# A two-pass feed-forward layer: ScalarE's order written out, more places for its activations, its first two blocks prepared inside attention

## The chip, the cores and the metric

The kernel runs on one core of a Trainium2 chip. The metric is the device time of one execution in microseconds (us). The engines of the core are called by the names that the profile uses: PE (TensorE, matmul; PEld is its weight load), DVE (VectorE), ACT (ScalarE), POOL (GpSimd) and SP (SyncE, which issues DMAs). Each engine works through its own queue in order and waits on semaphores that other engines raise. PE writes to PSUM, which has eight banks of 128 x 512 words; in what follows a "bank" is one of these.

## The reference, cut to what matters

The input is x of 4 batches x 1024 tokens x 128. Four layers follow one another, each added to x, each on a layer norm of x:

1. an attention layer with 16 heads,
2. a feed-forward layer with ternary weights, the one that the change rewrites,
3. a gated linear attention, which first needs a decay for each token,
4. a mixture of experts, of which three of eight are taken for each batch.

```python
def _L0_ffn_ref(x, w1_w, w1_s, w2_w, w2_s, h1_w, h1_s, h2_w, h2_s, w3_w, w3_s):
    h = jax.nn.silu(_tlin(x, w1_w, w1_s)) * _tlin(x, w2_w, w2_s)
    h = jax.nn.gelu(_tlin(h, h1_w, h1_s), approximate=False)
    h = jax.nn.gelu(_tlin(h, h2_w, h2_s), approximate=False)
    return _tlin(h, w3_w, w3_s)          # _tlin: x @ w.T * s
# 128 -> 512 (w1, w2), 512 -> 512 (h1), 512 -> 512 (h2), 512 -> 128 (w3)
# decay of the layer after it, from the x that this layer leaves:
gk = jax.nn.log_sigmoid(x @ Wgk1 @ Wgk2 + bgk2) / 16
```

## The kernel before, in words

**Attention.** Its scores are worked off in 16 sets of 16 steps. In each step PE makes two tiles of maxima (`mx`) for the set after, two tiles of scores (`sc`) and the weighted sums (`oacc`); DVE reduces the maxima (`nm`, L367), ACT takes the exponential (`pr`, L564). PE's order is the order of the program text (`manual_schedule`), that of the other engines is chosen by a scheduler. Small pieces of other work go into two queues, `after` and `ahead`, and `others()` (L514) takes at most one piece that needs PSUM per step. All these pieces share one bank (`misc`). Before each half of a batch, `prepare` norms, turns and projects its tokens; the projection (L290) keeps a tile under the tag `raw`, of which there are two places. In the last half there is nothing left to prepare, and `turn_pieces` turns the weights of the feed-forward layer there.

**The two-pass layer** (`ffn0_rounded`, L673) runs after a branch on a flag. Ternary weights are exact in a rounded format, so each activation is split into a high part (`*_hi`, a rounded copy) and a low part (`*_lo`, the rest), and each product is made twice. The 4096 tokens are 8 blocks of 512. For each block there are

- `turn` (L718): norm, four transposes (`tps`), `x_hi` on ACT, `x_lo` on DVE;
- `gates` (L736): for each of four column groups 4 matmuls, tanh on ACT (`sg`, L743), two products on DVE (`sg`, L744, and `h`, L746), `h_hi` on ACT, `h_lo` on POOL;
- `hidden` (L757), once for h1 and once for h2: 32 matmuls into four banks, then four gelus on ACT (`g`, L766) with two places for `g`, `g_hi` on ACT for groups 0 and 2 and on DVE for 1 and 3, `g_lo` on POOL for groups 0 to 2 and on DVE for 3;
- `down` (L777): 8 matmuls, `yT` on ACT, and later four transposes (`yps`, L812) and the sum into x;
- `behind`, the decays of the next layer (`gla_decay`, L1014), in three pieces: `turn` (norm, transposes `dps`, copy `h_nat`), `rank` (`lps`, `lr` on ACT), `decays` (`zps`, `low` on DVE, then absolute value on ACT, and for every second block an exponential and a logarithm of 1024 columns, a subtraction on POOL and two scans on DVE, `g_sum`).

Seven banks hold the matmul results of `gates`, `hidden` and `down`. One bank (`ps_t`, tag `turn`) is shared by `tps`, `yps`, `dps`, `lps` and `zps`.

The loop is skewed. Iteration k makes h2 of block k, h1 of block k+1, w3 of block k and the gates of block k+2. The small pieces wait in a queue `later`, and `hidden` takes one of them after each quarter of its matmuls. So an iteration from 1 to 5 has `yps`, `tps`, nothing, `dps` in h2 and nothing, `lps`, nothing, `zps` in h1. The pieces that come from block k-1 make iterations 2, 4 and 6 "heavy" (they hold the exponential and logarithm of a whole batch); 1, 3 and 5 are "light". Iteration 7 and the tail behind the loop each have the exponential and logarithm of half a batch. PE's order is the program's; ACT, DVE and POOL are ordered by the scheduler.

Of the kernel before, what the change touches and what calls it, by code (L numbers as in the profile page):

```python
# [9 lines left out]
F32 = mybir.dt.float32  # L10
# [14 lines left out]
class Block:  # L25
# [35 lines left out]
    def load_later_weights(self):  # L61
# [3 lines left out]
        for name in ("w1", "w2", "h1", "h2", "w3"):  # L65
# [9 lines left out]
            for name, t in self.ffn0_w.items()  # L75
        }
        self.same = self.ctile([P, 512], "same")
        nc.gpsimd.memset(self.same, 1.0)
# [45 lines left out]
    def turn_pieces(self, bank):  # L124
# [14 lines left out]
        for name, nat in self.ffn0_w.items():  # L139
            for ic in range(nat.shape[2] // P):  # L140
                out.append(
                    lambda k=len(out), nat=nat, dst=self.ffn0_r[name], ic=ic: piece(k, nat, dst, ic)
                )
        return out

    def set_flag(self, work, bank):
# [38 lines left out]
    def attention(self):  # L185
# [7 lines left out]
        with ExitStack() as ctx:  # L193
# [330 lines left out]
            for s, (hf, i) in enumerate(sets):  # L524
                cur = halves[hf]
                if i == 0 and hf + 1 < n_half:
                    halves[hf + 1], todo = prepare(hf + 1)
                    for piece in todo:
                        ahead.append(piece)
                        if hf > 0 and piece[0] and compare:  # L530
                            ahead.append((0, compare.pop(0)))
                elif i == 0:
                    ahead.extend((1, f) for f in self.turn_pieces(misc))
                    ahead.append((1, lambda: self.set_flag(work, misc)))
                qf = cur["q"][:, i].rearrange("p c t -> p (c t)")
# [42 lines left out]
            weighted(pend)  # L578
            while after:
                after.popleft()[1]()  # L580

# [91 lines left out]
    def ffn0_rounded(self, behind):  # L673
# [7 lines left out]
        with ExitStack() as ctx:  # L681
# [3 lines left out]
            ps_m = ctx.enter_context(tc.tile_pool(name="r_psm", bufs=7, space=PSUM))  # L685
            ctx.enter_context(tc.manual_schedule(engines={mybir.EngineType.PE}))

# [48 lines left out]
            def gates(x2):  # L736
                out = []
                for oc in range(FC):
                    gate, val = bank(), bank()
                    products("w1", {oc: gate}, x2, 0, 1)  # L740
                    products("w2", {oc: val}, x2, 0, 1)
                    sg = work.tile([P, TB], F32, name="sg", tag="sg")
                    nc.scalar.activation(sg, gate, AF.Tanh, scale=half[:, oc : oc + 1])  # L743
                    nc.vector.scalar_tensor_tensor(sg, sg, 1.0, gate, ALU.add, ALU.mult)  # L744
# [10 lines left out]
            later = deque()  # L755

            def hidden(name, src):  # L757
                out = {oc: bank() for oc in range(FC)}
                for ic in range(FC):
                    products(name, out, src[ic], ic, FC)  # L760
                    if later:
                        later.popleft()()
                res = []
                for oc in range(FC):
                    g = work.tile([P, TB], F32, name="g", tag="g")
                    nc.scalar.activation(g, out[oc], AF.Gelu, scale=col(name, oc))  # L766
# [10 lines left out]
            def down(blk, g):  # L777
# [4 lines left out]
                nc.scalar.mul(yT, ps[0], col("w3", 0))  # L782
                return [lambda: self.add_turned(ps_t, yT, 4 * blk), lambda: None] + behind(blk, ps_t)
# [38 lines left out]
    def gla(self):  # L822
# [3 lines left out]
        with ExitStack() as ctx:  # L826
# [83 lines left out]
            for b in range(B):  # L910
# [15 lines left out]
                for a in range(4):  # L926
                    qhs = []
                    for jq in range(4):
                        j = 4 * jq + a
                        kv = work.tile([P, S], F32, name="kv", tag="kv")  # L930
                        for hb in range(NH):
# [9 lines left out]
                            nc.vector.tensor_tensor(kv[:, cols], vr, kT[:, cols], ALU.mult)  # L941
                        hs = work.tile([P, S], F32, name="hs", tag="hs")
                        nc.vector.tensor_tensor_scan(hs, dec, kv, 0.0, ALU.mult, ALU.add)
# [70 lines left out]
    def gla_decay(self, blk, pool, ps_pool):  # L1014
# [48 lines left out]

        return [turn, lambda: None, rank, lambda: None, decays]

# [460 lines left out]
```

## Time and profile before

| what | us |
|---|---|
| median of three runs (1667.61 to 1690.93) | 1667.72 |
| the profiled execution | 1665.73 |
| its span, from the first to the last instruction | 1664.0 |
| of it, attention and what leads up to it, to the last `ctxT` product at 982.3 | 982 |
| the two-pass layer with the decays, 982.3 to 1282.5 | 300 |
| the gated linear attention and the experts | 381 |

The views of the profile show one execution. Times count from the start of the span. A row of the timeline is a start, a length, the engine, the line, the operation with its tiles, and in brackets the idle time ahead of it with what ended it. A row of the windows is the stretch, its length, the busy time of each engine with its number of instructions, and the PE clock that was granted (1.00 is full), the share of the DMA engines and the GB/s moved.

### The profile page before, as it was taken

To read this page: it belongs to the slowest core of one execution; us is meant where nothing else is said; L and a number is where in the kernel's file an instruction comes from. 1 tells how busy PE (TensorE), PEld (TensorE's weight loads), DVE (VectorE), ACT (ScalarE), POOL (GpSimd) and SP (SyncE) were. 2 spreads that over 40 slices of the span, in tenths; PEclk is the share of its full clock that TensorE was granted. 3 is DMA by queue.
4 is the path that set the end of the run, shared out by engine and by line. 5 is a ranking of instruction groups with operands and counts; after the bars stand their busy time and mean duration, and the time that the engine had idled before them with its cause. 6 is when DMAs were issued, how large, how long until landed. Compare 5 with 4: busy or idle time off the path is not lost. (4 is left out here: it accounts for less than half of the span.)

```text
span 1664.0 us, 25053 instructions
## 1 busy us (share of the span) xinstructions
PE 1400.1 (84%) x10256; PEld 712.5 (43%) x10256; DVE 1068.9 (64%) x1863; ACT 843.9 (51%) x1053; POOL 490.0 (29%) x469
## 2 busy tenths in 40 slices
PE   1599887799898998998989969979774878679998
PEld 1343333334343343433433326656551544445554
DVE  3688795689898897988988736643442555532220
ACT  0056663466666666666666645555544323153332
POOL 4434066525051150421500016544442000201110
PEclk9999997899999999999999989979895987789999
DMA  5000000000000000000000000000000000101110
GB/s 140 4 2 1 1 1 1 0 2 2 1 2 1 2 2 1 1 1 1 2 1 1 1 1 0 1 1 1 0 0 2 1 1 1 30 10 51 51 51 15
DMA packets 23247, 16.06 MB, mean 10 GB/s; under 512 B 9536, under 2 KB 20432, under 8 KB 23120
## 3 DMA queue, kind: packets, MB, share of 16 engines
q1 hardware_dynamic: 15792, 7.99, 1.7%
q0 software_dynamic: 1920, 6.29, 1.4%
q8 instruction: 84, 1.38, 0.4%
q10 hardware_dynamic: 5408, 0.05, 0.2%
q14 instruction: 43, 0.35, 0.1%
HBM read 12.23 MB, written 2.10 MB: 9 GB/s over the span
## 5 line engine op out<-in xcount | busy, mean ns | idle before, releaser
L564 ACT ACTIVATE pr<-sc 128x1024 f32<-128x1024 f32 x512 | 518.1, 1026 | 321.9 <-PE sc L556 272.1
L367 DVE TENSOR_REDUCE nm<-mx 128x2 f32<-128x1024 f32 x512 | 612.8, 1219 | 106.1 <-PE sc L556 57.6
L360 PE MATMUL mx<-k,q 32*128 32x512 f32 x1024 | 264.1, 516 | 53.6 <-ACT pr L564 40.3
L477 PE MATMUL oacc<-pr,vaug 128*32 128x512 f32 x2048 | 280.8, 617 | 0.0
L547 PE MATMUL sc<-q,k 32*128 32x512 f32 x1024 | 251.6, 502 | 22.7 <-DVE nm L367 21.0
L547 PEld LDWEIGHTS sc<-q,k 32*128 32x128 f32 x1024 | 95.4, 185 | 291.2 <-issue 107.2
L556 PE MATMUL sc<-mT,a_ones 32*128 32x512 f32 x1024 | 201.8, 394 | 0.0
L360 PEld LDWEIGHTS mx<-k,q 32*128 32x128 f32 x1024 | 97.3, 189 | 127.0 <-ACT pr L564 105.1
L165 POOL TENSOR_TENSOR ln_rs<-ln_rs,mhalf 128x4 f32<-128x4 f32 (+2 forms) x44 | 42.5, 967 | 313.2 <-DVE ln_rs L164 312.8
L1459 ACT ACTIVATE g<-up 128x512 f32<-128x512 f32 x96 | 56.7, 597 | 105.3 <-PE up L1451 105.2
L1451 PE MATMUL up<-mT,wa 128*128 128x512 f32 x192 | 97.8, 599 | 0.4 <-DVE att_s L1207 0.4
L556 PEld LDWEIGHTS sc<-mT,a_ones 32*128 32x128 f32 x1024 | 97.6, 189 | 0.6 <-ACT mT L378 0.2
L1441 PE MATMUL zT<-g,wb 128*128 128x512 f32 x192 | 97.4, 602 | 0.0
L773 POOL TENSOR_TENSOR g_lo<-g,g_hi 128x512 fp32r<-128x512 f32 x48 | 65.4, 1375 | 73.0 <-ACT g_hi L771 60.0
L386 POOL COPY mxpad<-mhi 128x16 f32<-128x16 f32 x32 | 6.8, 212 | 263.4 <-PE sc L556 179.0
L769 DVE CAST g_hi<-g 128x512 fp32r<-128x512 f32 x32 | 16.9, 528 | 94.8 <-ACT g L766 94.8
L314 POOL TENSOR_SCALAR raw<-raw,wq_take 128x512 f32<-128x512 f32 x32 | 50.2, 1569 | 82.8 <-DVE hi L313 81.5
L1451 PEld LDWEIGHTS up<-mT,wa 128*128 128x128 f32 x192 | 58.6, 309 | 31.8 <-issue 19.4
L477 PEld LDWEIGHTS oacc<-pr,vaug 128*32 128x32 f32 x2048 | 41.4, 108 | 70.2 <-issue 68.2
L766 ACT ACTIVATE g<-mm,h_s 128x512 f32<-128x512 f32 x64 | 42.3, 687 | 56.6 <-POOL g_lo L773 29.1
L314 POOL TENSOR_SCALAR raw<-raw,wk_take 128x512 f32<-128x512 f32 x32 | 50.5, 1579 | 33.4 <-DVE hi L313 33.4
L710 PE MATMUL mm<-g_hi,h_r 128*128 128x512 f32 x128 | 47.3, 475 | 10.6 <-DVE sg L744 4.6
(244 smaller groups left out, 2004.8 us busy)
## 6 DMA issues: line engine op xcount, KB each, us to landing
xs<-in_L_attn_x SPq DMA_DIRECT2D x8, 256.0 KB
h_nat<-in_L_ffn_h_w SPq DMA_DIRECT2D x2, 1024.0 KB
out<-xs SPq DMA_DIRECT2D x8, 256.0 KB
w_nat<-in_L_ffn_w_w SPq DMA_DIRECT2D x3, 256.0 KB
bq<-in_L_attn_bq ACTq DMA_DIRECT2D x16, 0.5 KB
bk<-in_L_attn_bk ACTq DMA_DIRECT2D x16, 0.5 KB
gWo<-in_L_attn_Wo SPq DMA_DIRECT2D x16, 4.0 KB
wa<-in_L_ffn_Wa,at_i POOLq DMA_INDIRECT x12, 3.7
```

The lines of the kernel that those rows point to most:

```text
L314: nc.gpsimd.tensor_scalar(raw, raw, take[key], None, ALU.mult)
L360: nc.tensor.matmul(ps[:, jj, :], qf[32 * j : 32 * j + 32, ch * P : (ch + 1) * P], kf[32 * j : 32 * j + 32, kh * KH : (kh + 1) * KH], start ...
L367: nc.vector.tensor_reduce(nm[:, kh, ch, 2 * jp : 2 * jp + 2], ps, AX.X, ALU.max, negate=True)
L477: nc.tensor.matmul(pend["oacc"][32 * j : 32 * j + 32, :], pend["v"][:, j, pend["ch"], :], pend["p"][j // 2][:, j % 2, :], start=pend["ch"] ...
L547: nc.tensor.matmul(ps[:, jj, :], kf[rows, ch * P : (ch + 1) * P], qf[rows, qh * KH : (qh + 1) * KH], start=True, stop=False,)
L556: nc.tensor.matmul(ps[:, jj, :], ones[rows, :], mT[rows, qh * KH : (qh + 1) * KH], start=False, stop=True,)
L564: nc.scalar.activation(pr, ps, AF.Exp, scale=scale)
L710: nc.tensor.matmul(ps, wT[name][:, ic, oc * P : (oc + 1) * P], half, start=ic == 0 and h == 0, stop=ic == n_ic - 1 and h == 1,)
L773: eng.tensor_tensor(g2[1], g, g2[0].bitcast(F32), ALU.subtract)
L1441: nc.tensor.matmul(zT, zones[k][1][:, fc * E : (fc + 1) * E], g, start=n == 0, stop=n == len(steps) - 1,)
L1451: nc.tensor.matmul(ps, zones[k][0][:, fc, :], xT[:, hb * TB : (hb + 1) * TB], start=True, stop=True,)
L1459: nc.scalar.activation(g, ps, AF.Gelu_apprx_tanh)
```

## The change

Five things are done.

1. In `ffn0_rounded` ACT, too, runs in the order of the program text.
2. `sg` gets three places instead of two, `h` four instead of two, `g` five instead of two. In `gates` the split of h into high and low part is put off by two column groups.
3. The queue `later` is gone. h2 of iteration k takes `yps` (of block k-1) after its first quarter and `dps` after its fourth; h1 takes `tps` (for block k+2) after its first quarter, `lps` after its second and `zps` with all that follows after its fourth. In the last iteration `lps` and `zps` come ahead of w3.
4. The norm, turn and split of blocks 0 and 1 move into the last half of attention (`first_pieces`), into four tiles of their own. Their normed tiles use the tag `raw`. In the queue `ahead` the two norms stand first, then the 14 turns of weights, then the two turns and the flag. Behind the last set both queues are emptied.
5. In `gla`, which stands on the side of a branch that is not taken here, `kv` and `hs` get one place instead of two.

```diff
+    def first_pieces(self, work, bank):
+        nc, out = self.nc, []
+        for blk, x2 in enumerate(self.first_x):
+            src = self.xs[:, 4 * blk : 4 * blk + 4, :]
+            got = {}
+            def norm(src=src, got=got):
+                mv, rs = self.norm_stats(work, src, 4)
+                got["xn"] = xn = work.tile([P, 4, E], F32, name="xn", tag="raw")
+                for k in range(4):
+                    self.norm_apply(xn[:, k, :], src[:, k, :], mv, rs, k)
+            def turn(x2=x2, got=got):
+                ps = bank()
+                for k in range(4):
+                    nc.tensor.transpose(ps[:, k * P : (k + 1) * P], got["xn"][:, k, :], self.ident)
+                nc.scalar.copy(x2[0], ps)
+                nc.vector.tensor_tensor(x2[1], ps, x2[0].bitcast(F32), ALU.subtract)
+            out += [(0, norm), (1, turn)]
+        return out[0::2] + out[1::2]
...
                 elif i == 0:
+                    first = self.first_pieces(work, misc)
+                    ahead.extend(first[:2])
                     ahead.extend((1, f) for f in self.turn_pieces(misc))
+                    ahead.extend(first[2:])
                     ahead.append((1, lambda: self.set_flag(work, misc)))
...
-            ctx.enter_context(tc.manual_schedule(engines={mybir.EngineType.PE}))
+            ctx.enter_context(
+                tc.manual_schedule(
+                    engines={mybir.EngineType.PE, mybir.EngineType.Activation}
+                )
+            )
...
-                    sg = work.tile([P, TB], F32, name="sg", tag="sg")
+                    sg = work.tile([P, TB], F32, name="sg", tag="sg", bufs=3)
...
-                    h = work.tile([P, TB], F32, name="h", tag="h")
+                    h = work.tile([P, TB], F32, name="h", tag="h", bufs=4)
...
-                    nc.scalar.copy(h2[0], h)
-                    nc.gpsimd.tensor_tensor(h2[1], h, h2[0].bitcast(F32), ALU.subtract)
+                    def cast(h=h, h2=h2):
+                        nc.scalar.copy(h2[0], h)
+                        nc.gpsimd.tensor_tensor(h2[1], h, h2[0].bitcast(F32), ALU.subtract)
+                    casts.append(cast)
+                    if oc >= 2:
+                        casts.popleft()()
                     out.append(h2)
+                while casts:
+                    casts.popleft()()
...
-            def hidden(name, src):
+            def hidden(name, src, slots):
                 out = {oc: bank() for oc in range(FC)}
                 for ic in range(FC):
                     products(name, out, src[ic], ic, FC)
-                    if later:
-                        later.popleft()()
+                    if slots[ic]:
+                        slots[ic]()
...
-                    g = work.tile([P, TB], F32, name="g", tag="g")
+                    g = work.tile([P, TB], F32, name="g", tag="g", bufs=5)
...
-            for blk in range(2):
-                piece, x2 = turn(blk)
-                piece()
-                turned[blk] = x2
-            h = {0: gates(turned.pop(0))}
-            g1 = {0: hidden("h1", h.pop(0))}
-            h[1] = gates(turned.pop(1))
+            h = {0: gates(self.first_x[0])}
+            g1 = {0: hidden("h1", h.pop(0), none)}
+            h[1] = gates(self.first_x[1])
+            add, decays = None, [None] * 3
             for blk in range(n_blocks):
+                piece = None
                 if blk + 2 < n_blocks:
                     piece, turned[blk + 2] = turn(blk + 2)
-                    later.insert(min(1, len(later)), piece)
-                g2 = hidden("h2", g1.pop(blk))
+                g2 = hidden("h2", g1.pop(blk), [add, None, None, decays[0]])
                 if blk + 1 < n_blocks:
-                    g1[blk + 1] = hidden("h1", h.pop(blk + 1))
-                more = down(blk, g2)
+                    g1[blk + 1] = hidden("h1", h.pop(blk + 1), [piece, decays[1], None, decays[2]])
+                else:
+                    decays[1]()
+                    decays[2]()
+                add = down(blk, g2)
+                decays = behind(blk, ps_t)
                 if blk + 2 < n_blocks:
                     h[blk + 2] = gates(turned.pop(blk + 2))
-                later.extend(more)
-            while later:
-                later.popleft()()
+            add()
+            for f in decays:
+                f()
...
-        return [turn, lambda: None, rank, lambda: None, decays]
+        return [turn, rank, decays]
```

More of the change, by code (lines that the diff above doesn't have):

```diff
@@ L76, in load_later_weights @@
         }
+        self.first_x = [
+            [self.ctile([P, 512], f"first{blk}_{h}", F32R) for h in ("hi", "lo")]
+            for blk in range(2)
+        ]
         self.same = self.ctile([P, 512], "same")
@@ L578, in attention @@
             weighted(pend)
-            while after:
-                after.popleft()[1]()
+            for queue in (ahead, after):
+                while queue:
+                    queue.popleft()[1]()
     def turned_norm(self, pool, ps_pool, src, tag, n, keep=None):
@@ L736, in gates @@
             def gates(x2):
-                out = []
+                out, casts = [], deque()
                 for oc in range(FC):
@@ L749, in gates @@
                     h2 = halves("h", 5)
-                    nc.scalar.copy(h2[0], h)
-                    nc.gpsimd.tensor_tensor(h2[1], h, h2[0].bitcast(F32), ALU.subtract)
+                    def cast(h=h, h2=h2):
[4 more added lines that the diff above has]
+                        casts.popleft()()
                     out.append(h2)
-                return out
-            later = deque()
-            def hidden(name, src):
+                while casts:
+                    casts.popleft()()
+                return out
+            def hidden(name, src, slots):
                 out = {oc: bank() for oc in range(FC)}
@@ L782, in down @@
                 nc.scalar.mul(yT, ps[0], col("w3", 0))
-                return [lambda: self.add_turned(ps_t, yT, 4 * blk), lambda: None] + behind(blk, ps_t)
+                return lambda: self.add_turned(ps_t, yT, 4 * blk)
+            none = [None] * FC
             turned = {}
-            for blk in range(2):
-                piece, x2 = turn(blk)
-                piece()
-                turned[blk] = x2
-            h = {0: gates(turned.pop(0))}
-            g1 = {0: hidden("h1", h.pop(0))}
-            h[1] = gates(turned.pop(1))
+            h = {0: gates(self.first_x[0])}
+            g1 = {0: hidden("h1", h.pop(0), none)}
+            h[1] = gates(self.first_x[1])
+            add, decays = None, [None] * 3
             for blk in range(n_blocks):
+                piece = None
                 if blk + 2 < n_blocks:
                     piece, turned[blk + 2] = turn(blk + 2)
-                    later.insert(min(1, len(later)), piece)
-                g2 = hidden("h2", g1.pop(blk))
+                g2 = hidden("h2", g1.pop(blk), [add, None, None, decays[0]])
                 if blk + 1 < n_blocks:
-                    g1[blk + 1] = hidden("h1", h.pop(blk + 1))
-                more = down(blk, g2)
+                    g1[blk + 1] = hidden("h1", h.pop(blk + 1), [piece, decays[1], None, decays[2]])
[4 more added lines that the diff above has]
+                decays = behind(blk, ps_t)
                 if blk + 2 < n_blocks:
                     h[blk + 2] = gates(turned.pop(blk + 2))
-                later.extend(more)
-            while later:
-                later.popleft()()
+            add()
+            for f in decays:
+                f()
     def add_turned(self, ps_pool, yT, n0):
@@ L929, in gla @@
                         j = 4 * jq + a
-                        kv = work.tile([P, S], F32, name="kv", tag="kv")
+                        kv = work.tile([P, S], F32, name="kv", tag="kv", bufs=1)
                         for hb in range(NH):
@@ L941, in gla @@
                             nc.vector.tensor_tensor(kv[:, cols], vr, kT[:, cols], ALU.mult)
-                        hs = work.tile([P, S], F32, name="hs", tag="hs")
+                        hs = work.tile([P, S], F32, name="hs", tag="hs", bufs=1)
                         nc.vector.tensor_tensor_scan(hs, dec, kv, 0.0, ALU.mult, ALU.add)
```

## The prediction

> **What bounds the kernel now.** I read the slices of the page first, then busy time by stage, then the waits and the timeline of the layer that is rewritten. By stage (before, core 0; stretch, length, busy time per engine, granted PE clock):
>
> ```profile
> 90.00:977.00 887.00, 803.19 (x7488) 339.98 (x7486) 729.82 (x1007) 552.41 (x601) 277.84 (x288) 0.98 0.01 1
> 977.00:1284.00 307.00, 230.82 (x848) 156.74 (x844) 144.14 (x371) 152.96 (x231) 135.64 (x111) 0.84 0.00 1
> ```
>
> Attention keeps PE busy for 91% and DVE for 82%: work added there has little cover. In the two-pass layer PE is busy for 75% at a mean clock of 0.84, and no other engine passes 50%: it is bound by a chain through several engines. The waits of that stage, in order of their sums, hold this line of ACT for POOL:
>
> ```profile
> ACT g L766 <- POOL g_lo L773: 29.1, 27, 2.9
> ```
>
> 27 gelus waited for one of two places of `g`. Is that wait on the path? A light iteration tells; ACT, from 1051 us on:
>
> ```profile
> 1052.35 0.62 ACT L771 CAST g_hi<-g 128x512 fp32r<-128x512 f32 x1
> 1052.86 0.60 ACT L1032 COPY h_nat<-dps 128x512 f32<-128x512 f32 x1
> ...
> 1060.10 1.27 ACT L766 ACTIVATE g<-mm,h_s 128x512 f32<-128x512 f32 x2 [2.65 <-PE mm L710]
> ...
> 1063.28 0.69 ACT L766 ACTIVATE g<-mm,h_s 128x512 f32<-128x512 f32 x1 [1.41 <-POOL g_lo L773]
> 1063.87 0.68 ACT L1050 ACTIVATE dec<-zps,gbgk 128x512 f32<-128x512 f32 x1
> ...
> 1066.10 1.28 ACT L743 ACTIVATE sg<-mm,r_half 128x512 f32<-128x512 f32 x2
> ```
>
> The scheduler fills the waits for POOL with `h_nat` and `dec`; the gelus go first, the decay work slips between them. PE's timeline says what the iteration turns on: in a heavy one it stops three times, for banks that ACT and DVE hold:
>
> ```profile
> 1096.90 0.79 PE L710 MATMUL mm<-x_hi,w_r 128*128 128x512 f32 x1 [3.44 <-ACT g L766]
> 1099.84 0.80 PE L710 MATMUL mm<-x_hi,w_r 128*128 128x512 f32 x1 [1.73 <-ACT yT L782]
> 1104.62 0.79 PE L710 MATMUL mm<-x_hi,w_r 128*128 128x512 f32 x1 [3.55 <-DVE sg L744]
> ```
>
> The head of the layer (DVE) waits for the norms of blocks 0 and 1:
>
> ```profile
> 987.44 0.29 DVE L161 BATCH_NORM_STATS2 ln_st<-xs 128x6 f32<-128x128 f32 x1 [1.62 <-POOL xs L468]
> ...
> 990.14 1.11 DVE L169 TENSOR_SCALAR xn<-xs,ln_mv,ln_rs 128x128 f32<-128x128 f32 x4 [0.84 <-POOL ln_rs L165]
> ...
> 998.16 0.68 DVE L744 SCALAR_TENSOR_TENSOR sg<-sg,mm 128x512 f32<-128x512 f32 x1
> ```
>
> I call DVE's first `sg` product (L744) of a group of gates the gate start. In the timeline it falls at 998.16 (block 0), 1013.71, 1039.99, 1067.41, 1103.91, 1134.47, 1173.61 and 1203.50 (block 7). Iterations 1 to 5 thus take 27.42, 36.50, 30.56, 39.14 and 29.89 us, and the tail, to the flag at 1282.54, 79.04.
>
> **Part by part: attention.** Two norms come in: 8 statistics of 285 ns, 8 aggregates of 158, 2 small ones of 197 and 8 applications of 365 make 6.9 us of DVE, with two powers of 0.97 on POOL, 8 transposes on PE (0.35 per four in the stream), two 0.59 casts on ACT, two 0.69 subtractions on DVE. The compiled order puts the 8 applications between the maxima at the end of the last projection, near 827, where DVE has no gap. The fifth needs the second `raw` place, free only when POOL has made `k` from it (it ends 3.1 us after DVE's `hi`); behind it in DVE's queue are the maxima that free PE's banks. That is 2.9 us of work and about 1 of waiting, which I charge to PE at 3; of the scattered statistics I charge 1, of the last set 1. Bounds 1 (DVE's idle share takes it) and 9 (all of it, and the misc bank behind); nothing leaves attention, so no gain; I take 5. SP's queue is unchanged and no DMA is moved.
>
> **The head.** Gone are two norms, transposes and splits. But DVE still waits for POOL's last `xs` (987.4), and its compiled order has the norm of block 2 ahead of the first gates: it is as far as the row before 992 us, against 998.16. PE's first gates need only `first_hi`, so they wait behind nothing but the branch. Then h1 of block 0, POOL's four `h_lo` of 1.30 and a power: gelu near 1004.3 against 1009.39. Its four gelus now run through, where the scheduler had put two tanhs between them; DVE starts the gates of block 1 4.95 us after the first gelu: 1009.2 against 1013.71, so 4.5 gained. In iteration 0 the places end the wait for sg of group 2 (1.9), and the gates start 4.35 us after h1 instead of 6.62: 26.28 becomes 22.1, 4.2 gained. Head: -8.7.
>
> **Light iterations.** Gate start to end of h2 was 11.63 (to `dps`, 1051.62). `tps` leaves h2 (0.35), and the third `sg` no longer stands behind `h_hi`, which frees the fourth bank 0.6 earlier: 10.65. Then h1, 8.99 before (to `zps`, 1060.61). ACT's order is now `h_nat`, four gelus with two casts, `x_hi`. From `dps`: 0.60 + 0.60 to the end of `h_nat`, gelus to 4.85 (0.58 each when the next does not depend on it, 0.69 when it does, casts alike), `x_hi` to 5.4; `x_lo`, behind `g_hi` and `g_lo` of group 3 on DVE, to 6.65. Until then the shared bank holds `tps`, and `lps` stands in PE's queue only one quarter behind it, at 4.55: PE waits 2.1, and all of h1 behind it. With `tps` h1 takes 11.5. Then ACT does `dec` before the gelus of h1: `zps` 1.16, `low` 0.75, `dec` 0.68 put the first gelu 2.53 after h1, where it had been 0.5 before its end. From there four gelus, two casts, `yT` and the first tanh run without POOL: 4.95 instead of 7.3. So 7.5 instead of 6.80. Sum 29.65, +2.2 for 27.42.
>
> **Heavy iterations.** Ahead of the gelus stand also three table loads of 1.283, an exponential and a logarithm of 1.06: 6.0. Gate start 2.53 + 6.0 + 4.95 = 13.5 after h1 instead of 15.88 (1088.03 to 1103.91), since before, two scans on DVE and a fourth load came ahead of it. 10.65 + 11.5 + 13.5 = 35.65: -0.85 for 36.50; the same for iteration 4. Iterations 3 and 5 lose the +2.2 but save the gelu table load that opened them (1.28): +0.95 each. Sum of 1 to 5: 2.2 - 0.85 + 0.95 - 0.85 + 0.95 = +2.4.
>
> Two rules of the Trainium skill bear on this. "ScalarE: Activation LUTs", rules for kernel authors, budgets some 2.7 us for each change of table set; the rows say 1.283. By the rule three loads ahead of the gelus would make the heavy iterations 4.2 longer and the sum +11; I take the row. "TensorE: Matmul & The Clock Gate", Part 1, says that an idle window of about 3.4 us halves PE's clock, and as long a busy one brings it back; it speaks against `lps` one quarter behind `tps`. Here the clock stood at 1.00 in 1093 to 1096, 0.56 in 1096 to 1099 and 0.50 until 1111, behind the 3.44 us gap; the 2.1 us wait stays short of it. Without a fall it costs as above, with one about 4 more per iteration.
>
> **Tail.** From the gate start of block 7: 10.65 to the end of h2, 9.8 for h1 (its fourth bank waits 0.8 for a gelu that is behind `h_nat`), 8.5 to the gelu (with the exponential): at 29.0. h2 of block 7 ends 11.7 later at a cold start (0.43 per matmul at half clock); before, PE waited 1.9 in it for `dps`. Then `dps`, `h_nat`, gelus, `lr`, `zps`, `dec`, two loads, two half activations, and only then `yT`, 12.6 after h2 (8.5 before). But `yps` then finds its bank free; before:
>
> ```profile
> 1255.39 0.69 ACT L782 ACTIVATE yT<-mm,w_s 128x512 f32<-128x512 f32 x1 [3.54 <-PE mm L710]
> ...
> 1260.38 1.12 PE L812 MATMUL yps<-ident,yT 128*128 128x128 f32 x4 [1.56 <-ACT dec L1050]
> ```
>
> From `yps` to the flag 22.1 before, less the 1.95 that the power stood behind POOL's `low`: 20.15. Sum 29.0 + 44.5 = 73.5, -5.5. What follows the flag keeps its order on every engine.
>
> **Sum.** +5 - 8.7 + 2.4 - 5.5 = -6.8, so a span of 1657. The profiled execution's 1665.73 lies 1.73 over its span and 2.0 under the median: 1661.
>
> **Rivals.** (a) This sum, 1661: 0.50. (b) `lps` finds its bank, as ACT is ahead of my count, and attention hides its additions at 1: five waits of 2.2 and 4 less, 1646: 0.17. For it speaks the 18% of DVE that is idle in attention; against, that PE is at 9.6 to 10 of 10 where the applications fall. (c) Slower: the wait for `lps` reaches an idle window, PE's clock falls once more in each of iterations 1 to 5, at about 4 each (8 us at half clock): 1681. It decides where the wait grows from 2.1 to 3.4, which one late `x_lo` behind `xn` on DVE would do. 0.23. (d) The change doesn't do what it says: a fixed ScalarE order is no shorter than the scheduler's, iteration 0 and the tail gain nothing: 5 - 4.5 + 2.4 = +2.9, 1671: 0.10. For it speaks that `dec` now holds gelus up; against, that POOL's wait is gone.
>
> **Numbers.** The range holds (a) with attention's bounds and (b), and reaches to (c): 1645 to 1682. 2% is about what a measurement of this kernel tells from no change; none of the cases but an extreme passes it: faster 0.04, same 0.89, slower 0.07.
>
> **What would show it.** The waits of the layer should lose "g from POOL" and hold PE's `lps` for DVE's `x_lo` at about 2.1 us, five times; gate starts should be 29 to 30 apart in light iterations and 35 to 36 in heavy ones; the first at 992 plus attention's loss; `yT` of block 7 behind the logarithm. The prediction is wrong if `nm` in the last half of attention stalls PE by over 9 us, or if the PE clock in light iterations is under 0.85.

## The result, and the profile after

The changed kernel took 1730.07 us (median of 4 runs, 1717.38 to 1734.92); the kernel before, on the same chip, 1673.36 us (4 runs). The ratio is 1.031, with a 95% interval from 1.021 to 1.041: slower. Executions more than 1.5% above the fastest of the same kernel, lengthened by falls of PE's clock, are left out of this and all ratios below (two of e8's four; the profiles of e2, e5 and e9 show such executions, with long falls in attention).

The profiled execution took 1726.58 us, with a span of 1724.6 against 1664.0: 60.6 us more. By stage (PE, PEld, DVE, ACT and POOL busy, each with its instructions; granted PE clock, DMA share, GB/s), attention and then the two-pass layer of the changed kernel:

```profile
90.00:1012.50 922.50, 834.62 (x7498) 348.86 (x7494) 735.08 (x1035) 554.29 (x603) 279.93 (x290) 0.93 0.01 1
1012.50:1345.00 332.50, 249.21 (x838) 164.79 (x836) 166.02 (x343) 146.59 (x225) 133.96 (x109) 0.81 0.00 1
```

Attention's clock fell from 0.98 to 0.93, the layer's from 0.84 to 0.81, and both stages became longer. The gate starts, as the prediction defines them, are 1026.54, 1044.70, 1069.93, 1105.95, 1150.03, 1187.64, 1229.88 and 1266.14 us, with the flag at 1343.38. By them the 60.6 us divide so:

| part | before | after | difference | predicted |
|---|---|---|---|---|
| attention's last product ends | 977.9 | 1012.5 | +34.7 | +5 |
| to the first gate start | 20.3 | 14.0 | -6.3 | -6.2 |
| gates of block 0 to block 1 | 15.55 | 18.16 | +2.6 | +1.7 |
| iteration 0 | 26.28 | 25.23 | -1.05 | -4.2 |
| iterations 1 to 5 | 163.5 | 196.2 | +32.7 | +2.4 |
| tail | 79.0 | 77.2 | -1.8 | -5.5 |

In the waits of iterations 1 to 5 (1069 to 1267 us), the gelus of the changed kernel no longer wait for POOL. PE waits at `lps` instead (us in sum, times, longest; the view found no releaser for one of the five, and calls it "issue"):

```profile
PE lps L1080 <- DVE x_lo L767: 11.7, 4, 3.3
PE lps L1080 <- issue: 3.6, 1, 3.6
```

Before, `lps` found its bank free, as `tps` was done with it in h2. The first of the five, and the products of h1 behind it, at full clock:

```profile
1055.80 1.03 PE L1036 MATMUL lps<-h_nat,gWgk 128*16 128x512 f32 x2
1056.76 1.19 PE L710 MATMUL mm<-h_hi,h_r 128*128 128x512 f32 x4
```

A light iteration shows what happens now. The timeline of the changed kernel from 1083 us:

```profile
1083.61 0.60 PE L765 MATMUL tps<-ident,xn 128*128 128x128 f32 x4
...
1084.51 3.08 DVE L196 TENSOR_SCALAR xn<-xs,ln_mv,ln_rs 128x128 f32<-128x128 f32 x4
...
1084.73 2.52 POOL L815 TENSOR_TENSOR g_lo<-g,g_hi 128x512 fp32r<-128x512 f32 x2 [0.43 <-DVE g_hi L811]
...
1085.24 0.58 ACT L766 CAST x_hi<-tps 128x512 fp32r<-128x512 f32 x1
...
1088.29 0.69 DVE L815 TENSOR_TENSOR g_lo<-g,g_hi 128x512 fp32r<-128x512 f32 x1
1088.89 0.68 DVE L767 TENSOR_TENSOR x_lo<-tps,x_hi 128x512 fp32r<-128x512 f32 x1
...
1089.68 1.87 PE L1080 MATMUL lps<-h_nat,gWgk 128*16 128x512 f32 x2 [3.60 <-issue]
...
1091.47 2.07 PE L745 MATMUL mm<-h_hi,h_r 128*128 128x512 f32 x4
```

`x_hi` is ready at 1085.8, but `x_lo` is behind four applications of a later norm, which take 3.08 us against POOL's `g_lo` (1.1 us otherwise). So the shared bank is free only at 1089.6, and PE stands still in front of `lps` for 3.60 us. Behind that the clock is halved: `lps` takes 1.87 us instead of 1.03, and four products 2.07 instead of 1.19. All five iterations have this stand, of 3.60, 3.31, 3.31, 2.55 and 2.55 us: 15.3 in sum.

The `xn` are not all of it. In iterations 4 and 5 none stands ahead of `x_lo`, as no further block has to be normed, and PE still waits 2.55 us. Iteration 4:

```profile
1204.08 2.69 POOL L815 TENSOR_TENSOR g_lo<-g,g_hi 128x512 fp32r<-128x512 f32 x2 [0.43 <-DVE g_hi L811]
1204.73 0.93 DVE L811 CAST g_hi<-g 128x512 fp32r<-128x512 f32 x1 [0.79 <-ACT g L808]
1205.69 1.63 DVE L815 TENSOR_TENSOR g_lo<-g,g_hi 128x512 fp32r<-128x512 f32 x1
1207.24 0.68 DVE L767 TENSOR_TENSOR x_lo<-tps,x_hi 128x512 fp32r<-128x512 f32 x1
1207.98 1.80 PE L1080 MATMUL lps<-h_nat,gWgk 128*16 128x512 f32 x2 [2.55 <-DVE x_lo L767]
```

Here DVE's own `g_hi` and `g_lo` are slow beside POOL's `g_lo`: 0.93 and 1.63 us, where away from it they take some 0.4 and 0.69. Whatever of DVE's work meets POOL's `g_lo` is held, and `x_lo` is behind it.

In the last of the three steps of an iteration, the one before the gates, DVE is late for the same reason:

```profile
1102.79 2.69 POOL L815 TENSOR_TENSOR g_lo<-g,g_hi 128x512 fp32r<-128x512 f32 x2 [0.36 <-DVE g_hi L811]
...
1104.38 1.65 DVE L815 TENSOR_TENSOR g_lo<-g,g_hi 128x512 fp32r<-128x512 f32 x1
1105.95 1.27 DVE L779 SCALAR_TENSOR_TENSOR sg<-sg,mm 128x512 f32<-128x512 f32 x2
```

DVE's `g_lo` of h2, in the light iteration above, took 0.69 us. This one, of h1, takes 1.65, until after POOL's second one has ended, and the gates are behind it.

Attention's 34.7 us have two causes. Three of its work units (from one transpose of `o` to the next) run at a fallen clock. The middle one of them before, and the three after:

```profile
529.86:556.52 26.66, 22.24 (x168) 8.30 (x168) 20.90 (x23) 16.81 (x18) 0.38 (x2) 1.00 0.00 1
```

```profile
502.99:536.41 33.42, 30.52 (x206) 11.33 (x206) 22.93 (x33) 17.46 (x19) 5.29 (x8) 0.73 0.00 1
536.41:576.75 40.34, 35.89 (x171) 11.79 (x169) 20.99 (x23) 16.85 (x18) 0.38 (x2) 0.50 0.00 1
576.75:607.64 30.89, 29.57 (x244) 12.36 (x242) 25.21 (x44) 17.93 (x20) 9.26 (x11) 0.84 0.01 1
```

These units hold nothing of the change. They took 104.65 us for 82.44: 22.2 of the loss. The rest is where the change is: the unit with the applications of the norms took 35.26 us instead of 27.16, the last one 20.24 instead of 16.24. Small differences of both signs make up the remainder.

### The profile page after: what moved, and what is told of

Same layout as the page of the kernel before. It is cut to its first block, busy times and chain, and to the rows that moved or that the text cites. A ratio compares the mean times of both kernels' runs of the same rounds, so it can differ in the third digit from the quotient of the medians.

```text
span 1724.6 us, 25037 instructions
## 1 busy us (share of the span) xinstructions
PE 1449.6 (84%) x10256; PEld 729.1 (42%) x10256; DVE 1095.9 (64%) x1863; ACT 839.3 (49%) x1049; POOL 490.8 (28%) x469
## 4 chain that ended last, share of the span: by engine, by line
PE 54%; DVE 23%; ACT 8%; issue 7%; POOL 6%; DMA 2%; ACTq 0%; POOLq 0%; SPq 0%; DVEq 0%
DVE nm L394 11%; PE oacc L504 10%; PE mm L745 7%; PE sc L577 7%; PE zT L1485 5%; PE up L1495 5%; PE mx L387 4%; ACT pr L594 4%; PE sc L586 3%; DVE raw L331 2%; PE misc L323 1%; DVE att_s L1251 1%; POOL raw L341 1%; DVE hi L340 1%; ACT g L808 1%
## 5 line engine op out<-in xcount | busy, mean ns | idle before, releaser
L387 PE MATMUL mx<-k,q 32*128 32x512 f32 x1024 | 273.9, 536 | 54.7 <-ACT pr L594 41.3
L504 PE MATMUL oacc<-pr,vaug 128*32 128x512 f32 x2048 | 294.5, 647 | 0.0
L577 PE MATMUL sc<-q,k 32*128 32x512 f32 x1024 | 260.5, 518 | 25.4 <-DVE nm L394 24.0
L586 PE MATMUL sc<-mT,a_ones 32*128 32x512 f32 x1024 | 209.1, 409 | 0.0
L586 PEld LDWEIGHTS sc<-mT,a_ones 32*128 32x128 f32 x1024 | 102.9, 198 | 1.5 <-ACT mT L405 0.2
L1495 PEld LDWEIGHTS up<-mT,wa 128*128 128x128 f32 x192 | 58.6, 309 | 31.8 <-issue 19.4
L811 DVE CAST g_hi<-g 128x512 fp32r<-128x512 f32 x32 | 25.1, 791 | 54.5 <-ACT g L808 54.5
L323 PE MATMUL misc<-xnT,wq_pad 128*32 128x128 f32 x1024 | 38.3, 295 | 18.3 <-ACT xnT L315 15.8
```

The costliest lines, as they stand in the source:

```text
L387: nc.tensor.matmul(ps[:, jj, :], qf[32 * j : 32 * j + 32, ch * P : (ch + 1) * P], kf[32 * j : 32 * j + 32, kh * KH : (kh + 1) * KH], start ...
L504: nc.tensor.matmul(pend["oacc"][32 * j : 32 * j + 32, :], pend["v"][:, j, pend["ch"], :], pend["p"][j // 2][:, j % 2, :], start=pend["ch"] ...
L577: nc.tensor.matmul(ps[:, jj, :], kf[rows, ch * P : (ch + 1) * P], qf[rows, qh * KH : (qh + 1) * KH], start=True, stop=False,)
L586: nc.tensor.matmul(ps[:, jj, :], ones[rows, :], mT[rows, qh * KH : (qh + 1) * KH], start=False, stop=True,)
L1495: nc.tensor.matmul(ps, zones[k][0][:, fc, :], xT[:, hb * TB : (hb + 1) * TB], start=True, stop=True,)
```

## The experiments

Two theories were to be told apart. Bank: PE stands at `lps`, because `tps` in the slot ahead holds the shared bank until DVE's late `x_lo`; the clock falls behind it. ScalarE: the fixed order costs, as it has `dec` and the table loads ahead of h1's gelus. A third question was what of attention's loss comes from the change. The measure is the three steps of iterations 1 to 5, each summed over the five: A, gate start to the start of `dps`; B, from there to `zps`, which is h1; C, from there to the next gate start.

| kernel | A | B | C | sum | ratio to before (95%) |
|---|---|---|---|---|---|
| before | 65.2 | 46.2 | 52.1 | 163.5 | 1 |
| changed | 58.6 | 80.5 | 57.1 | 196.2 | 1.031 (1.021 to 1.041) |
| e5 before, places only | 57.3 | 45.0 | 40.9 | 143.2 | 0.984 (0.979 to 0.990) |
| e12 before, slots only | 62.9 | 69.3 | 52.1 | 184.3 | 1.010 (1.000 to 1.021) |
| e3 changed, ScalarE free | 54.2 | 62.3 | 40.8 | 157.3 | 0.993 (0.989 to 0.996) |
| e2 changed, lps first | 59.8 | 52.1 | 57.1 | 169.0 | 1.002 (0.998 to 1.007) |
| e6 e3 and e2 together | 55.3 | 47.9 | 40.8 | 144.0 | 0.983 (0.978 to 0.988) |
| e4 changed, DVE fixed | 69.3 | 68.9 | 57.1 | 195.3 | 1.012 (1.001 to 1.023) |
| e10 changed, decays late | 52.8 | 79.6 | 28.3 | 160.6 | 0.992 (0.989 to 0.996) |
| e8 e10 and lps first | 52.8 | 54.9 | 28.4 | 136.1 | 0.974 (0.968 to 0.980) |

### e1: the changed kernel again

No edit.

> The changed kernel once more, unaltered, to see what of its loss comes back. In its first profile 22.5 us of the 60.6 us were lost in attention at 517 to 587 us, where nothing was changed: PE's clock fell to 0.50 behind a 1.00 us wait for nm that the kernel before has too (there the clock was back after 3.3 us). Theory chance: such a fall lasts differently in each execution; the stretch will be found at another length or place, attention ends near 990 and the span is 1700 to 1735. Theory layout (the added tiles cause it): attention ends again at 1010 within 2 us, with 0.50 from 518 to 587. Both: iterations 1 to 5 of the layer again 196 us within 5, with lps waiting about 3.5 us for x_lo.

Measured: 1712.45 us (4 runs, 1697.45 to 1722.25), ratio 1.020 (1.005 to 1.034). Attention ended at 992.4. The stretch near 520 us now ran at full clock, and a fall came in the two units from 609 to 672 us instead; the unit with the norms took 32.66 and the last one 20.27. Iterations 1 to 5 took 196.3 us, each within 0.1 us of its first time. So the long falls inside attention are chance in their places, and the loss of the layer is not. The kernel before has such falls too: its 84 runs beside the changed kernel and these experiments go from 1663 to 1711 us. One fall comes every time: the unit with the norms runs at a mean clock of 0.76 to 0.85 in all eight profiles that keep their normed tiles under `raw`.

### e5: places alone

```diff
 # before.py, ffn0_rounded
-sg = work.tile(..., tag="sg"); h = work.tile(..., tag="h"); g = work.tile(..., tag="g")
+sg = work.tile(..., tag="sg", bufs=3); h = work.tile(..., tag="h", bufs=4)
+g = work.tile(..., tag="g", bufs=5)
```

(To fit into the memory, two tiles of the branch that is not taken, `kv` and `hs`, get one place, as in the change.)

> The kernel before with nothing but the added places (3 for sg, 4 for h, 5 for g; the order of ScalarE and the slots as before). If the waits of the gelus for POOL's g_lo (29.1 us in sum) stood on the path, as the prediction's steps had it, iterations 1 to 5 fall from 163.5 us to 150 to 158 and the time to 1655 to 1664 in undisturbed runs. If the scheduler's fill-ins had made them free, they stay at 160 to 166. Attention is untouched: its work unit near 829 stays 27.2 and its last one 16.2.

Measured: 143.2 us; median 1650.06, the least run 1643.44. The wait for POOL was on the path, and the places alone are worth 20.3 us, more than I had expected. C falls by 11.3, A by 7.9. Which of the three tags is worth how much was not tried apart.

### e12: slots alone

```diff
 # before.py, ffn0_rounded: the queue `later` replaced by
+g2 = hidden("h2", ..., [add, None, None, decays[0]])
+g1[blk + 1] = hidden("h1", ..., [piece, decays[1], None, decays[2]])
```

> The kernel before with nothing but the set slots: tps and lps in the first two of h1, yps and dps in h2's, zps in h1's last; places, ScalarE's free order and the head as before. With the added places the same slots cost 14.1 us in iterations 1 to 5 (143.2 to 157.3). Theory bank alone: x_lo comes later still, as the gelus wait for POOL, the stand at lps is over 2 us, and the iterations take 172 to 185 instead of 163.5; the time is 1676 to 1692. Rival (PE waits at those places before the change too, so the stand only takes another's place): 160 to 168 and a time within 5 us of before.

Measured: 184.3 us, 20.8 more than before: B grew by 23.1 (46.2 to 69.3), A fell by 2.3, with stands at `lps` of 3.06, 3.11, 3.44, 1.81 and 2.14 us. The second one:

```profile
1096.68 0.68 DVE L764 TENSOR_TENSOR x_lo<-tps,x_hi 128x512 fp32r<-128x512 f32 x1
...
1097.51 1.57 PE L1072 MATMUL lps<-h_nat,gWgk 128*16 128x512 f32 x2 [3.11 <-DVE x_lo L764]
```

Theory bank holds for this part alone. The median, 1696.62, is above the expected range, with falls in attention in it; the least run, 1684.49, is inside.

### e3: ScalarE's order left to the scheduler

```diff
-engines={mybir.EngineType.PE, mybir.EngineType.Activation}
+engines={mybir.EngineType.PE}
```

> ScalarE's order is left to the scheduler again, all other parts stay; the compiled order then has dec behind the gelus of h1, h_nat between those of h2, and on DVE three of the four xn behind x_lo. Theory bank: lps still stands behind tps, but x_lo no longer behind four slowed xn: the wait falls to 2 us, short of a fall of the clock; iterations 1 to 5 take 165 to 178, and the time is 1697 to 1712. Theory ScalarE: the iterations are at or under the 163.5 of before, and the time under 1697.

Measured: 157.3 us; median 1661.06 over 20 runs, the least 1650.62. By its numbers theory ScalarE is met: A and C fall by 4.4 and 16.3, and C is that of e5. But B is still 17 above e5's, and the stand is there, at the size that theory bank gave it (1.93, 1.97, 1.97, 1.74, 1.74). It said that 2 us would stop short of a fall, and that was wrong: behind the first three the clock fell for 3.41 us, behind the two of 1.74 it did not. The second iteration of e3:

```profile
1083.34 1.51 PE L1080 MATMUL lps<-h_nat,gWgk 128*16 128x512 f32 x2 [1.97 <-DVE x_lo L767]
...
1084.78 2.08 PE L745 MATMUL mm<-h_hi,h_r 128*128 128x512 f32 x4
```

Two causes, then. The stand acts in B; ScalarE's order acts in A and C, and in B too, since with it free the stand shrinks from 2.55 to 3.60 us to 1.74 to 1.97.

### e2: lps ahead of tps

```diff
-[piece, decays[1], None, decays[2]]
+[decays[1], piece, None, decays[2]]
```

> Slots of h1 swapped: lps, then tps, nothing, zps; all else as changed. Theory bank (PE stands at lps until DVE's x_lo has freed the shared bank, long enough for the clock to fall): the wait for x_lo in front of lps is gone, zps finds its bank, PE's clock in the light iterations is over 0.95, and iterations 1 to 5 fall from 196 us to 160 to 170; the time falls by 25 to 35, to 1690 to 1705. Theory ScalarE (its fixed order, with dec and the table loads ahead of the gelus, is what costs): iterations stay over 185 and the time within 10 of the changed kernel's 1730.

Measured: 169.0 us, in theory bank's range; median 1685.01 over 20 runs, 5 us under it. The wait is gone from all five iterations (here the first):

```profile
1092.50 1.03 PE L1080 MATMUL lps<-h_nat,gWgk 128*16 128x512 f32 x2
```

B falls from 80.5 to 52.1: the stand cost 28.4 us, of which 15.3 are the waits and 13.1 the half clock behind them. The trace of the changed kernel bears this out: 27.8 us of its five B behind the waits are at half clock, and half of that, 13.9, is about the 13.1 (an estimate). C is unchanged to 0.1 us, and A is 1.2 longer. The clock of the light iterations was 1.00, 0.88 and 0.95, so not over 0.95 in each. Against the kernel before, B had grown by 34.3, so the stand makes most of the layer's 32.7; but ScalarE's free order alone (e3) takes back 38.9 of the 196.2, and lps ahead alone 27.2.

### e6: both

Edits of e2 and e3 together.

> ScalarE's order left to the scheduler and lps in the slot ahead of tps; places and attention's norms as changed. Theory bank: the five waits of 1.74 to 1.97 us that are left in front of lps with the free order go, and with them the cold matmuls behind two of them: iterations 1 to 5 fall from 157.3 to 143 to 150 us, undisturbed runs to 1638 to 1646. Rival (what PE gains there it waits for at the gates and the fourth bank instead): 153 to 158, runs at 1648 to 1654.

Measured: 144.0 us, median 1645.49, the least run 1638.57. As theory bank had it: B falls by 14.4, of which 9.35 are the waits and about 5 the three falls behind them. In the layer e6 is e5 with other slots, at the same 143 to 144 us.

### e4: DVE's order fixed too

```diff
-engines={mybir.EngineType.PE, mybir.EngineType.Activation}
+engines={mybir.EngineType.PE, mybir.EngineType.Activation, mybir.EngineType.DVE}
```

> DVE's order in the layer is fixed as well, which puts the four xn of the next block ahead of h2's work, away from POOL's g_lo; lps stays behind tps. Theory contention (xn takes 3.08 instead of 1.1 us while POOL runs g_lo, and x_lo is late by that): x_lo comes 2 to 3 us earlier, lps waits 0.5 to 1.5, the clock in light iterations is over 0.9, iterations 1 to 5 take 165 to 175. Theory place (x_lo is late because g_hi and g_lo of the last group stand ahead of it, whatever xn does): lps waits over 2.5 and the iterations stay over 185. Both: dn may come up to 2 us later, since xn and its power are now ahead of it.

Measured: 195.3 us, no better. By its numbers theory place is met: the iterations stay over 185, and three of the stands are still 2.55. The four `xn` do take 1.11 us away from POOL's `g_lo`. But `x_lo` ends 8.5 us behind the start of `dps`, for 8.8 to 9.1 in the first three iterations of the changed kernel and 8.1 in the last two: now DVE's `g_hi` and `g_lo` of h2 meet POOL's `g_lo` instead. The second iteration:

```profile
1092.27 2.69 POOL L817 TENSOR_TENSOR g_lo<-g,g_hi 128x512 fp32r<-128x512 f32 x2 [0.43 <-PE mm L747]
...
1093.88 1.63 DVE L817 TENSOR_TENSOR g_lo<-g,g_hi 128x512 fp32r<-128x512 f32 x1
...
1096.17 1.03 PE L1082 MATMUL lps<-h_nat,gWgk 128*16 128x512 f32 x2 [2.55 <-DVE x_lo L769]
```

In iterations 1 and 3 the stand is 0.97 and 1.05, but not because `x_lo` is earlier: with `xn` and its power ahead, `xs` and `dn` came late, PE waited at `dps`, its clock fell to 0.50 for 3.41 us behind that, and so it came later to `lps`. The first iteration:

```profile
1046.83 1.11 DVE L196 TENSOR_SCALAR xn<-xs,ln_mv,ln_rs 128x128 f32<-128x128 f32 x4 [1.12 <-POOL ln_rs L192]
...
1051.51 1.05 PE L1077 MATMUL dps<-ident,dn 128*128 128x128 f32 x4 [1.62 <-issue]
...
1060.11 1.03 PE L1082 MATMUL lps<-h_nat,gWgk 128*16 128x512 f32 x2 [0.97 <-DVE x_lo L769]
```

B became 11.6 shorter and A 10.7 longer, so nearly all of the gain was given back.

### e10 and e8: the decay's activations late

```diff
 # gla_decay: decays() split into product() [zps], size() [low, dec], rest() [exp, ln, scan]
 g1[blk + 1] = hidden("h1", ..., [piece, decays[1], None, product])   # e8: [decays[1], piece, ...]
+size()                      # behind h1's gelus
 add = down(blk, g2)
 h[blk + 2] = gates(...)
+rest()                      # behind the next gates' tanhs and casts
```

> ScalarE's order fixed as in the changed kernel and lps ahead of tps, but dec is emitted behind h1's gelus, and the exponential and logarithm with their loads behind the tanhs and casts of the next gates. With lps ahead alone the iterations took 169.0 us, 12 more than with a free order behind tps. Theory decays (the rest of the fixed order's price is dec and the loads ahead of the gelus): 140 to 152 us, with heavy iterations under 33. Rival (it is h_nat and the casts between h2's gelus): over 158 us, light ones over 29.

> The changed kernel with the decay activations late as in e8, but tps ahead of lps as it was changed. It asks whether the two losses of iterations 1 to 5 add: the changed kernel 196.2 us, lps ahead alone 169.0, both mends 136.1. Theory additive (the stand at lps costs its 27 whatever ScalarE does): 158 to 166 us, waits of 2.5 to 3.6 for x_lo, clock fallen behind them. Rival (the stand grew to the point of a fall only because the gelus came late): 140 to 150 us and waits under 2.

Measured: e8 136.1 us, median 1651.02 over 4 runs, the least 1628.99, ratio 0.974 (0.968 to 0.980). C falls from 57.1 to 28.4, since the exponential and the logarithm with their two loads now run while PE does h2. ScalarE of e8 behind a heavy iteration:

```profile
1098.81 1.28 ACT L787 CAST h_hi<-h 128x512 fp32r<-128x512 f32 x2 [0.91 <-DVE h L781]
1100.11 1.28 ACT L1107 ACT_TABLE_LOAD   x1
...
1103.78 1.06 ACT L1108 ACTIVATE dec<-dec 128x1024 f32<-128x1024 f32 x1
1105.41 0.59 ACT L1080 COPY h_nat<-dps 128x512 f32<-128x512 f32 x1 [0.58 <-PE dps L1079]
```

ScalarE still waits 0.58 us for `dps` behind the logarithm: all but the third load, for the gelu, is hidden (that one shows in B, 11.82 for 10.41 in two iterations). PE's clock stays at 1.00 in all five iterations; the first three:

```profile
1040.92:1067.58 26.66, 24.95 (x102) 17.48 (x103) 18.34 (x41) 14.31 (x25) 15.10 (x12) 1.00 0.00 0
1067.58:1094.22 26.64, 25.65 (x106) 17.72 (x105) 17.86 (x35) 14.85 (x26) 14.12 (x11) 1.00 0.00 1
1094.22:1122.28 28.06, 25.67 (x106) 17.71 (x105) 22.06 (x38) 20.92 (x31) 17.80 (x13) 1.00 0.00 1
```

Heavy iterations now take 26.65 us like light ones, and those behind a heavy one 28.06; PE is busy for 25.7 of 26.65. e10, with `tps` ahead, has the stands again (3.60, 3.33, 4.00, 2.56 and 2.06) and B at 79.6: 160.6 us, in the additive theory's range. So with ScalarE's order fixed the stand costs 25 to 28 us of B whether the decays are early or late, and the two losses nearly add: 27.2 and 35.6 us apart, 60.1 together. With ScalarE free the stand costs 14.4 of B (e3 against e6). A fixed order of ScalarE is not dear in itself: with the decays late the iterations are 8 us shorter than under the scheduler (e6), and e8 is faster than both kernels. Late decays with ScalarE free were not tried, so it is open how much of the 8 us is the order and how much the place of the decays.

### e11: places of its own for the norms in attention

```diff
 # on e8, first_pieces
-xn = work.tile([P, 4, E], F32, name="xn", tag="raw")
+xn = work.tile([P, 4, E], F32, name="xn", tag="first_xn")
```

> e8 with two places of its own for the xn of attention's norms instead of those of raw; the compiled order then has these 8 applications and their small operations some sets earlier, scattered between maxima, and none near 829. Theory place (the unit near 829 lost 5.5 us because the fifth application waits for POOL's k, 1.2 us, and all fall into a stretch that DVE fills): the unit takes 27 to 28.5 instead of 32.6, and what is left is at most 2 us in the units that take them; attention ends 3 to 5 us earlier than in e8 where undisturbed. Rival (it is DVE's work itself, 2.9 us, wherever it is put): the 5 us turn up in the other units. Both: the last unit keeps its +4.0, since it is the transposes on PE and the shared misc bank.

Measured: ratio 0.978 (0.971 to 0.986). The unit near 829 took 27.16 us, at a clock of 1.00, instead of 32.66 at 0.84 in e8. The applications ran near 575 us instead, in two units that became 2.2 and 1.2 us longer without a fall. So of the 5.5 some 2.1 come from the place, with the clock, and 3.4 from the work, which goes along wherever it is put: each theory has a part. Whether attention ends earlier for it this profile cannot say, as long falls lie elsewhere in it. Iterations 1 to 5 took 140.0 us, 4 more than in e8, with two falls of the clock, though the edit does not touch them. How the place cost was seen in the profile after:

```profile
853.00 1.30 POOL L342 TENSOR_TENSOR k<-hi,raw 128x512 fp32r<-128x512 f32 x1
854.34 0.60 DVE L196 TENSOR_SCALAR xn<-xs,ln_mv,ln_rs 128x128 f32<-128x128 f32 x2 [1.21 <-POOL k L342]
...
856.13 0.50 PE L577 MATMUL sc<-q,k 32*128 32x512 f32 x2 [1.45 <-DVE nm L394]
```

The last unit kept its 20.27. In e8 it shows what the norms push into it, where before PE had only the scores and the products with `v`:

```profile
966.37 0.33 PE L136 MATMUL misc<-ident,w_nat 128*128 128x128 f32 x1
968.95 0.66 PE L166 MATMUL misc<-ident,xn 128*128 128x128 f32 x4
971.85 0.66 PE L166 MATMUL misc<-ident,xn 128*128 128x128 f32 x4
974.75 1.02 PE L176 MATMUL misc<-same,mhalf 128*1 128x512 f32 x2
```

As I read these rows, the two `misc` pieces more put the last turned weight and the flag into a unit that PE bounds; no run tests this alone.

### e7 and e9: nothing of the norms in attention

On e6 and on e8: `first_pieces` is not called, and blocks 0 and 1 are turned at the head of the layer as before.

> As the run before it, with blocks 0 and 1 turned at the head of the layer again and nothing of them in attention. Attention loses its additions, +5.5 us in the work unit near 829 and +4.0 in the last one: it ends 8 to 9 us earlier; the head becomes 6 us longer (first gates 21.4 us after attention's end instead of 14 to 15). So 2 to 3 us less in sum, iterations as in the run before it. Rival (those two units lost their time to a fall of PE's clock that would have come anyway): attention ends less than 4 us earlier and the sum is 2 us more.

> As e8 (ScalarE fixed, lps ahead of tps, dec behind h1's gelus, exponential and logarithm behind the next gates), with blocks 0 and 1 turned at the head of the layer and nothing of them in attention. By the units of attention in the runs so far its two additions cost 5.5 + 4.0 - 0.7 = 8.8 us and save 6.3 at the head: without them 2.5 less than e8, whose least run was 1629; so undisturbed runs at 1625 to 1628, iterations 1 to 5 136 us as in e8. Rival (the additions pay): 1630 or more.

Measured: e7 0.981 (0.974 to 0.987), least run 1636.15, against e6's 1638.57; e9 0.977 (0.971 to 0.983), least run 1630.39, against e8's 1628.99. The iterations are as in e6 and e8 (142.6 and 135.8). The last unit is back at 16.2, the head at 20.3 and 20.8. In e7 attention ended 5.4 us earlier than in e6 and the head was 6.3 longer. The other units hold falls of their own in both profiles, and the runs differ by less than the spread that the falls make. That the norms in attention cost more than they save, by 2 to 3 us, is argued from the units (5.5 + 4.0 - 0.7 against 6.3); the times neither show nor exclude it: e7's least run is 2.4 under e6's, as expected, but e9's is 1.4 over e8's, where its rival had it.

## Why the prediction was wrong

**Range and rivals.** 1730 lies outside 1645 to 1682, and so do the least of the 8 runs of the changed kernel, 1697, and the profiled run without the chance falls in attention, 1726.6 - 22.2 = 1704. Of the prediction's signs, "g from POOL" is gone and `lps` waits five times for `x_lo`, but 2.55 to 3.60 us instead of 2.1; the clock of the light iterations was 0.91, 0.82 and 0.86, once under its mark of 0.85. Rival (c), at 0.23, had the direction and the place, and its 4 us per iteration are near the 3.6 that the stand took beyond the 2.1 counted. Its point of decision, 3.4, lay too high, and its cause, "one late `x_lo` behind `xn` on DVE", covers only the part above 2.55.

**The step that failed is h1: "With `tps` h1 takes 11.5."** In five iterations that is 57.5; B measured 80.5. Of the 23.0 too little, 4.8 are longer waits (15.3 instead of five times 2.1) and 13.1 the half clock behind them. The other 5.1 are h1 without the stand: 10.42 each in e2, not the 9.4 counted. With ScalarE free it is 9.59 (e6), so 0.8 of it is the fixed order: the gelus stand behind `h_nat`, and h1's fourth bank comes late. I had charged that to the tail alone.

The wait was mis-sized in the term "`x_lo`, behind `g_hi` and `g_lo` of group 3 on DVE, to 6.65". Measured, `x_lo` ended 8.1 to 9.1 us behind the start of `dps`, while PE reached `lps` at 5.60 instead of 4.55. The sum took DVE's operations at their time alone. Beside POOL's `g_lo` the `g_hi` and `g_lo` of iterations 4 and 5 took 1.4 us more, which is about the whole way from 6.65 to 8.1; the four `xn` of the first three iterations, which the sum leaves out, bring it to 8.8 and 9.1.

**"The 2.1 us wait stays short of it"** was the second error. I weighed the clock by a threshold that no row of this kernel had shown. In iteration 4 PE stood for 2.55 us, and the clock was half in the stretch behind it:

```profile
1205.40:1208.00 2.60, 0.05 (x2) 0.02 (x2) 2.49 (x3) 0.00 (x0) 1.38 (x1) 1.00 0.00 0
1208.00:1211.00 3.00, 3.00 (x5) 1.20 (x6) 0.00 (x0) 0.57 (x1) 0.00 (x0) 0.52 0.00 0
```

**The step before the gates** was right in its first half: in the light iteration the first gelu came 2.53 us behind `zps`, as counted. From there to the gates it took 6.2 instead of 4.95, since DVE's `g_lo` and `g_hi` stand against POOL's (means over iterations 1 to 5 of 693 and 525 ns before, 1357 and 770 after). Light iterations 8.75 for 7.5, heavy ones 15.43 for 13.5: +7.6 in five. That `dec` and the loads ahead of the gelus cost was seen, but it was taken as given; e8 against e2 shows that this order alone was worth 28.7 us of C.

**Gate start to `dps`**: 10.65 was right where the iteration starts with a warm clock (10.55), and 1 to 1.6 too little in the four that start cold. In the sum this all but cancels: iterations 3 to 5 were counted as differences from before, and so kept 5.7 us of its cold starts. The sum for the five was thus 165.9, and 23.0 in h1, 7.6 before the gates and -0.3 here make the 30.3 that it fell short of 196.2.

**Attention.** The charge of 5 became 8.8 by the units: 5.5 for 3 + 1 (the wait for `raw` was 1.21, and a fall of the clock came on top), and 4.0 - 0.7 for the last set's 1. The bounds, 1 and 9, held. The 22.2 more of the profiled run are chance. Without them the change is 60.6 - 22.2 = 38.4 us, and the least of its 8 runs is 34 us above the least of before.

**Head.** The first gate start was right (997.1 to 998.3 in e3, e6 and e8, for 992 and attention's loss). Iteration 0 took 25.1 to 25.9 with ScalarE fixed (e4, with DVE fixed too, apart) and 23.0 to 23.3 with it free, for 22.1: the places alone (e5) gave 24.0, so a part of what was counted, and the fixed order gave most of that back.

**Tail.** `yT` of block 7 stands behind the logarithm, as foreseen. The gelus of block 7 came at 30.9 for 29.0, `yps` at 56.3 for 53.3, and the rest took 20.9 for 20.15. Of the first 1.9, 1.55 are the cold start of h2; this h1 has no `tps` and no stand, and took 9.97 for 9.8.

Rival (d), that a fixed order is no shorter than the scheduler's, was true of this order: 196.2 us against 157.3 in iterations 1 to 5.

## What to carry to other kernels

A bank that several users share is a queue: before moving one user ahead of another, add up all that stands before the operation that frees it, on each engine, each with its duration beside what the other engines do at that time. Fixing an engine's order takes away the scheduler's fill-ins; here it paid only once long operations that nobody waits for were emitted where that engine idles. Try the parts of a change one by one: here the places alone gained 20 us, the slots alone lost 21, and together, in e3, they left 6.

## What the runs showed of the hardware

**VectorE and GpSimd hold each other up.** One `xn` of 128x128 takes 0.34 us alone and up to 1.37 while POOL subtracts 128x512; DVE's `g_lo` takes 0.69 and up to 1.65. The gates' products `sg` and `h`, which read PSUM and one operand from SBUF, kept 0.67 to 0.69 and 0.74 to 0.75 beside POOL's `h_lo`. The Trainium skill ("SBUF — State Buffer", Who interferes with whom) says that a VectorE copy, cast or tensor-scalar in a two-port mode, or an operation with two SBUF inputs against a GpSimd read, shares a port pair under an exclusive lock, so that the later one waits for the whole of the other. The rows agree, though none shows the mode of an `xn`. The other way round it is POOL that waits. Before, DVE's `g_lo` began first and kept its time, and POOL's took 1.75 us where it takes 1.29 alone:

```profile
1056.81 0.69 DVE L773 TENSOR_TENSOR g_lo<-g,g_hi 128x512 fp32r<-128x512 f32 x1
1056.90 1.75 POOL L773 TENSOR_TENSOR g_lo<-g,g_hi 128x512 fp32r<-128x512 f32 x1 [1.30 <-PE lps L1036]
```

**PE's clock falls behind short waits, and can stay down.** The skill's "TensorE: Matmul & The Clock Gate", Part 1, names an idle window of some 3.4 us. Here the clock fell behind waits of 2.55, 1.97 and 1.93 us in the layer, and not behind two of 1.74. In attention it was half from 518.6 to 586.9 us behind one of 0.34 and one of 1.00:

```profile
516.00 0.49 PE L577 MATMUL sc<-q,k 32*128 32x512 f32 x2 [0.34 <-DVE nm L394]
517.73 0.50 PE L577 MATMUL sc<-q,k 32*128 32x512 f32 x2 [1.00 <-DVE nm L394]
```

The kernel before has the same two waits there; its clock was back after 3.4 us. By the measurement, not the rule, waits under 3.4 us count. That the state lasts because a PE at half speed, 36 of 40 us busy, still leaves gaps is argued, not shown; what sets its beginning in an execution stays open. One regularity is in the clock records of all fourteen profiles: within one execution every fall begins on a grid with steps of 3.41 us and lasts a whole number of steps, behind the five stands of the changed kernel two, in iteration 4 one. Where on that grid a wait lies may decide whether it counts; no run varied this.
